# A graph attention kernel's first projection: pairs of tiles multiplied by seven half products instead of eight

## The chip, the cores and the metric

The kernel runs on one core of a Trainium2 chip. The core has five engines that run side by side, each with its own in-order queue of instructions: TensorE (PE) multiplies matrices into PSUM, VectorE (DVE) and ScalarE (ACT) work on tiles of 128 partitions, GpSimd (POOL) does so too and issues the indirect DMAs (gathers and scatters by an index), and SyncE (SP) issues most other DMAs. Engines wait for each other through semaphores.

The metric is the device time of one execution in microseconds. Before the change its median is 5629.17 us over 13 runs, the lowest 5609.52, the highest 5641.94.

## The reference, cut to what matters

Two graph attention layers over N = 10000 nodes and 170000 edges (each node has an edge to itself), with norms and residuals:

```
h0 = x                                            # 10000 x 768, float32
xl    = x @ W1                                    # W1 768 x 1024: 4 heads of 256
a_src = sum over a head of xl * a_src1            # one number per node and head
a_dst = sum over a head of xl * a_dst1
e     = leaky_relu(a_src[src] + a_dst[dst], 0.2)
alpha = softmax of e over the edges with the same dst
h     = segment_sum(xl[src] * alpha, dst) + b1
h     = relu(layer_norm(h)) + h0 @ Wr1 + br1
... the second layer in the same way, with W2, Wr2 and one head of 768 ...
out   = layer_norm(x + h)
```

The list of edges comes sorted by `dst`.

## The kernel before, in words

Nodes are taken in tiles of 128; 10000 nodes are NT = 79 tiles, numbered 0 to 78. The program has three stages, one after the other: the projection (described here), `ordered_layer1` and `ordered_layer2`. Between the first and the others stands a branch: every engine reads the number `fits` (written at L421 by the last step of the sorting) and goes on only then (L1232, L1234).

**The projection** is the loop at L659. For tile t it multiplies the transposed x (`xT`, 128 x 6 x 128, loaded by SP in `load_x`, L615, three buffers, two tiles ahead) by `w1` (six blocks of 128 x 1024). `product` (L164) issues 12 matmuls of 128 x 512, six for each half of the 1024 columns, into one of two PSUM tiles `big`; all is float32, and the profile shows two PE records for each such matmul. Then, for the same tile:

- ACT copies the product from PSUM to `row` (L662);
- DVE multiplies the product by `ad_b` and then by `as_b` into `scr` (L665, two buffers), and ACT sums each of the 4 heads of both with an accumulating activation (L668, 8 of them);
- POOL adds the bias `b1_b` to `row` (L670);
- SP issues the load of x for tile t + 2 (L671) and stores `row` to the DRAM table `table1` (L672);
- `next(steps)` (L673) issues one more step of two other pieces of work.

The order within each engine is the order in which this Python code issues the instructions (`manual_schedule`).

**The steps** are two generators taken side by side, `prepare` first and then `weight_steps`.

`weight_steps` (L632) loads W2 and, in 16 steps, multiplies one block of it by an attention vector on DVE (L647) and sums it on ACT (L648); then it multiplies `br1` by W2 on PE (L651) and evicts that on ACT (L653).

`prepare` (L190) sorts the nodes by their number of edges and finds where each node's edges are. Its parts, in order, are: loading the ends of the edge list; eleven transposes on PE (L216); 27 steps of **counts**; a one-hot matrix `hot` and 79 running additions `before` on DVE (L271, L276); ranks (L323 to L330, PE and DVE, eight tiles at a time); **scatters** of 79 columns to `order_d` by POOL (L313, six in a step); four loads back and the store `less_rank` on SP (L344, L347); and 20 steps of **slots**: POOL gathers `window` for four tiles (L392) and DVE, a step later, works out the slots from them (`listed`, L365).

A step of counts (L235 to L250) does three counts, each a DVE comparison of 1408 numbers with an accumulated sum (L239); converts them to integers `at` (L241); POOL gathers three `chunk` rows by `at` (L244); and DVE counts within the chunks of the step before (`remainder`, L228).

Of the kernel before, what the change touches and what calls it, by code (L numbers as in the profile page):

```python
# [28 lines left out]
F32 = mybir.dt.float32  # L29
I32 = mybir.dt.int32  # L30
BF16 = mybir.dt.bfloat16
AF = mybir.ActivationFunctionType
OP = mybir.AluOpType
AX = mybir.AxisListType

P = 128
# [43 lines left out]
def gnn_kernel(ctx, tc, x, x_cols, src, dst, src_col, dst_col, W1, a_src1, a_dst1, b1, g1, be1, Wr1, br1,  # L80
# [109 lines left out]
    def prepare():  # L190

        with tc.tile_pool(name="prep", bufs=1, side="right") as pool, \
                tc.tile_pool(name="prep2", bufs=2, side="right") as pool2:
            rows = pool.tile([P, NA, P], I32, name="rows")
            nc.sync.dma_start(rows, bass.AP(tensor=dst.tensor, offset=0, ap=[[P, P], [P * P, NA], [1, P]]))
            nxt = pool.tile([P, NA, P], I32, name="nxt")
# [7 lines left out]
            fall = pool2.tile([P, NA * P], F32, name="less", bufs=1).rearrange("p (a e) -> p a e", e=P)  # L204
# [9 lines left out]
            for a in range(NA):  # L214
# [6 lines left out]
                           allow_small_or_imprecise_dtypes=True)  # L221
            whole = pool.tile([P, NB], F32, name="whole")
# [10 lines left out]

            asked = []
            for j in range(0, NB, STEP):  # L235
                m = min(STEP, NB - j)
                for i in range(j, j + m):
                    less = pool2.tile([P, NA * P], F32, name="less", bufs=1)
                    nc.vector.tensor_scalar(less, most.rearrange("p a e -> p (a e)"), ids[:, i:i + 1], 0.0,  # L239
                                            op0=OP.is_lt, op1=OP.add, accum_out=whole[:, i:i + 1])  # L240
# [32 lines left out]
            before = pool.tile([P, NT + 1, D], BF16, name="before")  # L273
# [12 lines left out]
            facts = pool.tile([P, NT, 4], I32, name="facts")  # L286
# [11 lines left out]
            while s < D:  # L298
                more = pool.tile([P, D], F32, name=f"more{s}")
# [20 lines left out]
            for j in range(0, NT, W):  # L320
# [4 lines left out]
                place = pool2.tile([P, W, D], F32, name="place", bufs=1)  # L325
# [15 lines left out]
            others = [pool.tile([P, NT, 4], I32, name=n) for n in ("rows", "nxt", "info")]  # L341
# [23 lines left out]
            def listed(t, window):  # L365
# [3 lines left out]
                have, got, eq = (pool2.tile(shape, F32, name=n, bufs=1)[:, :m, :k] for n in ("have", "got", "eq"))  # L369
# [237 lines left out]
    with tc.tile_pool(name="w1", bufs=1) as w1p, tc.tile_pool(name="l1", bufs=2) as io, \  # L607
            psum_for_products(), tc.manual_schedule():
# [3 lines left out]
        def load_x(t):  # L612
            if t < NT:
                xTs[t] = io.tile([P, K0, P], F32, name="xT", bufs=3)
                nc.sync.dma_start(xTs[t], x_cols[t])  # L615
# [4 lines left out]
        load_x(1)  # L620
# [11 lines left out]
        def weight_steps():  # L632
# [7 lines left out]
            brT = spread_br1(w1p, "brT")  # L640
# [10 lines left out]
            q = product(brT, w2, R2)  # L651
            row = io.tile([P, R1], F32, name="row")
            nc.scalar.copy(row[:, :R2], q[:, :R2])  # L653
# [5 lines left out]
        for t in range(NT):  # L659
            p = product(xTs.pop(t), w1, C1)  # L660
# [625 lines left out]
```

## Time and profile before

| what | value |
|---|---|
| median of 13 runs | 5629.17 us |
| the profiled execution | 5638.83 us, span 5637.0 us |
| mean granted TensorE clock | 0.924 |
| projection, first to last matmul of L171 with `xT` | 8.9 to 872.0 us |
| matmul records of the projection | 1896 (79 tiles x 12 x 2) |
| eviction L662 of tile 0 and of tile 78 | start at 23.12 and 872.63 us |
| DVE L665, 128 x 1024 | 1.22 us each |
| ACT L668, 128 x 256 with a sum | 0.40 us each |
| DVE count L239, 128 x 1408 | 1.68 us each, 80 of them |
| POOL bias addition L670 | 2.37 us each |
| first instruction of the next stage on POOL (L424) | 882.1 us |

How it is read: times are of one execution, counted from the start of the span. A line of a timeline gives the start, the duration, engine, line of the code, operation, output and inputs with their shapes, and in brackets how long the engine had been idle before it and what released it. A line of the stretches gives each engine's busy time in the stretch, then the clock that TensorE was granted (1.00 is full), the DMA engines' busy share and GB/s. "xN" merges N records that follow each other.

### The profile page before, as it was taken

The page shows a single profiled execution, that of the slowest core. Times are in us where ns is not written, and L with a number is a line of the kernel's source. Part 1 is how long each engine was busy: PE and PEld are TensorE (multiplying, and loading weights), DVE is VectorE, ACT ScalarE, POOL GpSimd, SP SyncE. Part 2 cuts the span into 40 slices and gives each one's busy share as a digit, 9 for nine tenths or more (in the row PEclk, how much of TensorE's full clock was granted, in tenths as well). Part 3 has the DMA queues.
Part 4 walks back from the last instruction along what each step waited for, and adds up shares of the span by engine and source line. Part 5 has one row for each costly group of instructions (what it writes and reads, how often), then busy time and mean ns, then how long its engine had stood idle before and what let it go on. Part 6 is the DMA issues. An engine that isn't in the chain of part 4 may idle for free. (4 is left out here: it accounts for less than half of the span.)

```text
span 5637.0 us, 59565 instructions
## 1 busy us (share of the span) xinstructions
PE 4915.2 (87%) x15188; PEld 2905.0 (52%) x15191; DVE 4289.6 (76%) x7729; ACT 2811.1 (50%) x8184; POOL 3243.1 (58%) x3159
## 2 busy tenths in 40 slices
PE   8999996999999866789999998998878758788898
PEld 3444443555555544455555555655555435455565
DVE  5883344999999887888999995886776566677787
ACT  3443344777787766778777772332222222222232
POOL 3447454556666655566666544666666556666563
PEclk9999997999999987899999999998888768888899
DMA  4333526899999986999999977988888878888885
GB/s 155 122 98 87 94 94 260 319 336 353 362 367 368 350 318 246 332 348 360 364 363 351 337 260 272 334 322 307 300 293 289 279 255 286 300 302 299 289 325 197
DMA packets 474306, 1591.37 MB, mean 282 GB/s; under 512 B 118327, under 2 KB 122487, under 8 KB 473958
## 3 DMA queue, kind: packets, MB, share of 16 engines
q0 software_dynamic: 322384, 1286.62, 64.0%
q1 hardware_dynamic: 149520, 297.43, 15.5%
q10 hardware_dynamic: 2054, 3.42, 0.2%
q8 instruction: 128, 2.10, 0.1%
q14 instruction: 220, 1.80, 0.1%
HBM read 1431.80 MB, written 177.29 MB: 285 GB/s over the span
## 5 line engine op out<-in xcount | busy, mean ns | idle before, releaser
L424 POOL DMA_INDIRECT ring<-table,slots x2675 | 2661.1, 995 | 1801.0 <-issue 531.9
L519 DVE SCALAR_TENSOR_TENSOR acc<-ring,e,acc 128x512 f32<-128x512 f32 (+1 forms) x2530 | 1578.3, 624 | 149.3 <-PE acc L733 45.4
L508 ACT ACTIVATE ring<-ring,e 128x256 f32<-128x256 f32 x3284 | 1338.3, 509 | 2.3 <-issue 2.2
L952 PE MATMUL big<-wr,w 128*128 128x512 f32 (+1 forms) x2464 | 905.7, 511 | 176.9 <-issue 175.3
L515 DVE TENSOR_TENSOR acc<-acc,ring 128x1024 f32<-128x1024 f32 x801 | 985.7, 1231 | 72.5 <-DVE acc L519 1.8
L938 PE MATMUL big<-ring,diagonals 128*128 128x256 f32 x2754 | 744.3, 430 | 170.3 <-issue 120.9
L171 PE MATMUL big<-w,xT 128*128 128x512 f32 x1896 | 823.8, 596 | 23.0 <-DMA w<-in_W_dram 10.3
L171 PE MATMUL big<-wr,xT 128*128 128x512 f32 x1896 | 832.5, 596 | 0.2 <-issue 0.2
L826 PE MATMUL half<-w,hT 128*128 128x512 f32 (+1 forms) x2528 | 830.4, 486 | 0.0
L952 PEld LDWEIGHTS big<-wr,w 128*128 128x128 f32 x2464 | 489.4, 200 | 556.9 <-issue 524.8
L938 PEld LDWEIGHTS big<-ring,diagonals 128*128 128x128 f32 x2754 | 589.9, 218 | 328.5 <-issue 193.5
L937 ACT ACTIVATE diagonals<-ident,e 128x128 f32<-128x128 f32 x1377 | 424.8, 388 | 648.8 <-remote 226.0
L826 PEld LDWEIGHTS half<-w,hT 128*128 128x128 f32 x2528 | 477.8, 189 | 372.3 <-issue 333.6
L733 PE MATMUL acc<-ring,diagonals 128*128 128x256 f32 x1912 | 479.3, 408 | 208.4 <-ACT diagonals L727 203.7
L171 PEld LDWEIGHTS big<-w,xT 128*128 128x128 f32 x1896 | 361.3, 191 | 481.0 <-issue 462.5
L171 PEld LDWEIGHTS big<-wr,xT 128*128 128x128 f32 x1896 | 356.6, 191 | 419.8 <-issue 419.8
L733 PEld LDWEIGHTS acc<-ring,diagonals 128*128 128x128 f32 x1912 | 386.7, 205 | 293.8 <-ACT diagonals L727 225.2
L581 ACT ACTIVATE sd<-mv,eps 128x1 f32<-128x1 f32 x237 | 69.4, 293 | 706.7 <-DVE mv L579 468.7
L727 ACT ACTIVATE diagonals<-ident,e 128x128 f32<-128x128 f32 x956 | 293.0, 387 | 204.7 <-DVE e L499 179.9
L665 DVE TENSOR_TENSOR scr<-big,ad_b 128x1024 f32<-128x1024 f32 x79 | 96.7, 1224 | 374.6 <-ACT row L662 311.1
L670 POOL TENSOR_TENSOR row<-row,none 128x1024 f32<-128x1024 f32 x79 | 187.3, 2370 | 259.4 <-ACT row L662 256.0
L485 ACT ACTIVATE e<-e 128x68 f32<-128x68 f32 (+29 forms) x160 | 38.2, 239 | 564.2 <-DVE e L484 313.2
(173 smaller groups left out, 3639.8 us busy)
## 6 DMA issues: line engine op xcount, KB each, us to landing
ring<-table,slots POOLq DMA_INDIRECT x2675
table<-row SPq DMA_DIRECT2D x79, 516.0 KB
h_d<-hT SPq DMA_DIRECT2D x79, 512.0 KB
w<-h_d SPq DMA_DIRECT2D x77, 512.0 KB
table<-row SPq DMA_DIRECT2D x79, 385.0 KB
ring<-table SPq DMA_DIRECT2D x79, 385.0 KB
xT<-in_x_cols_dram SPq DMA_DIRECT2D x79, 384.0 KB
x_d<-xt SPq DMA_DIRECT2D x79, 384.0 KB
```

The lines of the kernel that those rows point to most:

```text
L171: nc.tensor.matmul(p[:, c:e], aT[:, j, :], w[:, j, c:e], start=(j == 0), stop=(j == k - 1))
L424: nc.gpsimd.indirect_dma_start(out=to, out_offset=None, in_=table, in_offset=bass.IndirectOffsetOnAxis(ap=index, axis=0), **more)
L508: nc.scalar.activation(row[:, s], row[:, s], AF.Copy, scale=e[:, h:h + 1])
L515: nc.vector.tensor_add(acc[:, :c], acc[:, :c], row[:, :c])
L519: nc.vector.scalar_tensor_tensor(acc[:, s], row[:, s], e[:, h:h + 1], (acc if first is None else first)[:, s], op0=OP.mult, op1=OP.add)
L670: nc.gpsimd.tensor_add(row[:, :C1], row[:, :C1], b1_b)
L727: nc.scalar.activation(diagonals[:, k * H1 + i, :], ident, AF.Copy, scale=e[:, k, i:i + 1])
L733: nc.tensor.matmul(acc[:, c:d], diagonals[:, k * H1 + i, :], ring.slot(q + k)[:, c:d], start=(k == 0 and c % BANK == 0), stop=(k == m - 1 ...
L826: nc.tensor.matmul(q, hT[:, j, :], w2[:, j, c:c + q.shape[1]], start=(j == 0), stop=(j == K1 - 1))
L937: nc.scalar.activation(diagonals[:, k % G, :], ident, AF.Copy, scale=e[:, k, :])
L938: nc.tensor.matmul(to, diagonals[:, k % G, :], ring.slot(FIRST[t] + k)[:, ON_PE2:C2], start=False, stop=(k == n - 1), skip_group_check=True)
L952: nc.tensor.matmul(r[:, c:d], hT[:, j, :], wr2[:, j, c:d], start=False, stop=(j == K1 - 1 and d < C2), skip_group_check=True)
```

## The change

Tile 0 is multiplied as before (by halves of the columns). After it the tiles are taken in pairs (1, 2), (3, 4) to (77, 78). The two tiles' x and W1 form 2 x 2 blocks: x's blocks are a11, a12 (tile t, first and second 384 of the inner dimension) and a21, a22 (tile t + 1); W1's are b11, b12, b21, b22 (halves of the inner dimension by halves of the columns). A half product is one such block by one such block, three matmuls of 128 x 512. Eight half products give the pair's result; the change uses Strassen's form with seven, of sums of blocks. b12 - b22 and b21 - b11 replace b12 and b21 in place, three more sums are kept in `bsums` (DVE, once), and five sums of x's blocks are made for each pair on DVE (`sums`, in `pair`), one pair ahead. The half products land in PSUM tiles of one bank, six of them. Two are evicted by ACT into `row` (m5 and m2); all others are added to or subtracted from `row` by DVE. `finish` is what came after the product before; it now reads `row` instead of PSUM, and each step follows one `finish`, so two steps are issued in a pair.

x has four buffers instead of three and is loaded for the tiles t + 4 and t + 5 ahead of the pair's stores; `row` has four buffers instead of two. Counts are issued one step ahead of the conversion that uses them, and those with an even number run on ACT: an accumulating Sign and a small activation that turns the sum of signs into a count. This adds one step to `prepare`. Several tiles of the sorting share storage under common names. `br1`'s product goes to the new PSUM tiles, two banks one after the other.

```diff
-            rows = pool.tile([P, NA, P], I32, name="rows")
+            both = pool.tile([P, 2, NA, P], I32, name="hot")
+            rows, nxt = both[:, 0], both[:, 1]
...
+            halves = pool.tile([P, NB], F32, name="halves")
+            nc.vector.tensor_scalar_add(halves, ids, -0.5)
...
+            def counts(j):
+                for i in range(j, min(j + STEP, NB)):
+                    less = pool2.tile([P, NA * P], BF16, name="less")
+                    if i % 2:
+                        nc.vector.tensor_scalar(less, most.rearrange("p a e -> p (a e)"), ids[:, i:i + 1], 0.0,
+                                                op0=OP.is_lt, op1=OP.add, accum_out=whole[:, i:i + 1])
+                        continue
+                    nc.scalar.activation(less, most.rearrange("p a e -> p (a e)"), AF.Sign, scale=-1.0,
+                                         bias=halves[:, i:i + 1], accum_out=whole[:, i:i + 1])
+                    nc.scalar.activation(whole[:, i:i + 1], whole[:, i:i + 1], AF.Copy, bias=0.5 * NA * P, scale=0.5)
+
             asked = []
+            counts(0)
+            yield
             for j in range(0, NB, STEP):
                 m = min(STEP, NB - j)
-                for i in range(j, j + m):
-                    less = pool2.tile([P, NA * P], F32, name="less", bufs=1)
-                    nc.vector.tensor_scalar(less, most.rearrange("p a e -> p (a e)"), ids[:, i:i + 1], 0.0,
-                                            op0=OP.is_lt, op1=OP.add, accum_out=whole[:, i:i + 1])
+                counts(j + STEP)
                 nc.vector.tensor_copy(at[:, j:j + m], whole[:, j:j + m])
...
-            others = [pool.tile([P, NT, 4], I32, name=n) for n in ("rows", "nxt", "info")]
+            others = [pool.tile([P, NT, 4], I32, name=n) for n in ("hot", "most", "info")]
...
-                xTs[t] = io.tile([P, K0, P], F32, name="xT", bufs=3)
+                xTs[t] = io.tile([P, K0, P], F32, name="xT", bufs=4)
...
-        for t in range(NT):
-            p = product(xTs.pop(t), w1, C1)
-            row = io.tile([P, R1], F32, name="row")
-            nc.scalar.copy(row[:, :C1], p[:, :C1])
+        def finish(t, row):
             for i, vec in enumerate((ad_b, as_b)):
                 m = io.tile([P, C1], F32, name="scr")
-                nc.vector.tensor_mul(m, p[:, :C1], vec)
+                nc.vector.tensor_mul(m, row[:, :C1], vec)
                 for h in range(H1):
...
             nc.gpsimd.tensor_add(row[:, :C1], row[:, :C1], b1_b)
-            load_x(t + 2)
             nc.sync.dma_start(table1[t * P:(t + 1) * P, :R1 - 1], row[:, :R1 - 1])
...
+        def times(a, b, p=None):
+            to = ps_m.tile([P, BANK], F32, name="m")[:, :NH] if p is None else p
+            for k in range(a.shape[1]):
+                nc.tensor.matmul(to, a[:, k, :], b[:, k, :], start=(p is None and k == 0),
+                                 stop=(k == a.shape[1] - 1), skip_group_check=True)
+            return to
...
+        def pair(t):
+            a1, a2 = (xTs.pop(i) for i in (t, t + 1))
+            a11, a12, a21, a22 = (a[:, k, :] for a in (a1, a2) for k in (upper, lower))
+            sums = io.tile([P, 5, KH, P], F32, name="sums")
+            for i, (a, op, b) in enumerate(((a11, OP.add, a12), (a21, OP.add, a22), (a11, OP.add, a22),
+                                            (a21, OP.subtract, a11), (a12, OP.subtract, a22))):
+                nc.vector.tensor_tensor(sums[:, i], a, b, op=op)
+            return a11, a22, sums
+
+        ready = pair(1)
+        for t in range(1, NT, 2):
+            a11, a22, sums = ready
+            r1, r2 = new_row(), new_row()
+            m3 = times(a11, b12)
+            m5 = times(sums[:, 0], b22)
+            nc.scalar.copy(r1[:, right], m5)
+            m2 = times(sums[:, 1], b11)
+            nc.scalar.copy(r2[:, left], m2)
+            nc.vector.tensor_sub(r2[:, right], m3, r2[:, left])
+            m4 = times(a22, b21)
+            nc.vector.tensor_sub(r1[:, left], m4, r1[:, right])
+            nc.vector.tensor_add(r1[:, right], r1[:, right], m3)
+            nc.vector.tensor_add(r2[:, left], r2[:, left], m4)
+            load_x(t + 4)
+            load_x(t + 5)
+            if t + 2 < NT:
+                ready = pair(t + 2)
+            m1 = times(sums[:, 2], bsums[:, 0])
+            nc.vector.tensor_add(r2[:, right], r2[:, right], m1)
+            m6 = times(sums[:, 3], bsums[:, 1])
+            nc.vector.tensor_add(r2[:, right], r2[:, right], m6)
+            times(sums[:, 4], bsums[:, 2], m1)
+            finish(t + 1, r2)
+            nc.vector.tensor_add(r1[:, left], r1[:, left], m1)
+            next(steps, None)
+            finish(t, r1)
             next(steps, None)
```

The seventh half product is added by PE onto the fifth (m1) in the same PSUM tile, after DVE has added m1 alone to r2. The step issued after `finish(t + 1)` is called step A in the text that follows, the one after `finish(t)` step B.

## The prediction

> **What bounds the kernel now.** I read the page first, then busy time by stretch of the projection (tile 78's last product matmul is issued at 872 us), then the timeline engine by engine inside each stretch.
>
> ```profile
> span 5637.0 us, 59565 instructions
> ...
> PE 4915.2 (87%) x15188; PEld 2905.0 (52%) x15191; DVE 4289.6 (76%) x7729; ACT 2811.1 (50%) x8184; POOL 3243.1 (58%) x3159
> ```
> ```profile
> core 0: us, PE busy (x) PEld busy (x) DVE busy (x) ACT busy (x) POOL busy (x), PEclk, DMA share, GB/s
> ...
> 75.00:257.00 182.00, 174.50 (x411) 77.07 (x410) 147.79 (x190) 81.06 (x302) 87.49 (x64) 1.00 0.35 118
> 257.00:372.00 115.00, 115.00 (x269) 50.92 (x268) 92.30 (x119) 48.35 (x188) 57.67 (x43) 1.00 0.33 107
> ...
> 436.00:640.00 204.00, 203.89 (x481) 90.28 (x482) 60.57 (x69) 82.85 (x328) 121.04 (x97) 1.00 0.45 93
> 640.00:872.00 232.00, 228.31 (x530) 100.87 (x529) 108.12 (x437) 94.94 (x374) 127.59 (x101) 0.99 0.36 90
> ```
> The projection is bound by PE: busy 100% from 257 to 372 us. But DVE is busy 80% there and 81% in the stretch before, because the sorting's counts lie beside the product. The average of 76% hides that: after 436 us DVE has 30%. In the first stretch PE is already held up, and the timeline shows by what:
>
> ```profile
> 128.38 0.84 ACT L648 ACTIVATE scr<-scr 128x768 f32<-128x768 f32 x1 [5.02 <-DVE scr L647]
> 129.13 0.18 ACT L648 ACTIVATION_READ_ACCUMULATOR scr<-scr 128x1 f32 x1
> 129.22 0.99 ACT L662 COPY row<-big 128x1024 f32<-128x1024 f32 x1
> ```
> ```profile
> 176.05 1.22 DVE L665 TENSOR_TENSOR scr<-big,ad_b 128x1024 f32<-128x1024 f32 x1 [1.90 <-ACT row L662]
> ...
> 178.32 1.67 DVE L239 TENSOR_SCALAR_CACHE_REDUCE less<-most,ids 128x1408 f32<-128x1408 f32 x1
> ...
> 180.03 1.68 DVE L239 TENSOR_SCALAR_CACHE_REDUCE less<-most,ids 128x1408 f32<-128x1408 f32 x1
> ```
> ```profile
> 167.05 10.54 PE L171 MATMUL big<-w,xT 128*128 128x512 f32 x24 [0.91 <-PE big L171]
> 178.50 10.54 PE L171 MATMUL big<-w,xT 128*128 128x512 f32 x24 [0.91 <-PE big L171]
> ```
> ACT works in order, so the eviction (L662) stands behind the step's L648, which waited for DVE; DVE then waits for the eviction, and PE loses 0.91 us. A tile takes 11.45 us here, 10.30 where PE is free (24 records, 0.429 us each). Evictions queued behind a step's work on ACT are thus a real bound, and the change puts more there.
>
> **The change part by part.** Pairs are named by their first tile: 39 pairs, tiles 1 to 78. All durations are of the profiled execution (5638.83 us; 9.7 above the median 5629.17, so I carry a difference over to the median).
>
> *Removed.* A half product is 6 records x 0.429 = 2.57 us. A pair had 8 (20.6 us) and has 7: 18.0. If PE set the pace, 39 x 2.57 = 100 us would go.
>
> *Added on DVE, per pair.* Five sums of 384 columns at 0.55 us (row L230), starting 0.47 apart: 2.45. Seven operations on 512 columns at 0.69 (rows L326, L328), 0.60 apart, 0.72 where one reads the one before: 4.6. Four multiplications of 1024 at 1.14 apart as before: 4.7 (from SBUF now; L665 reads PSUM in 1.22, so I change nothing). That is 11.6 against 4.7 before. Evictions on ACT: two of 512 at 0.59 (row L706) for two of 1.01.
>
> *Counts.* 80 counts at 1.72 us (L239 start to start) lay on DVE; 40 stay. One on ACT: L668 is 0.40 for 256 columns and L648 0.84 for 768, so 1.39 for 1408; a per-partition operand adds 0.11 (L508 0.51 against 0.40), and a small Copy that waits for the accumulator 0.3: 1.8. Between 1.4 and 2.2. Step A (after tile t+1) has two counts on DVE and one on ACT, step B (after tile t) one and two.
>
> *The new waits.* The order within a pair is now: PE may start the seventh product only when DVE has added the fifth to r2; ahead of that add DVE has four additions, the five sums, and ahead of those the wait for ACT's eviction of the third product, which is queued behind step B. Going once round from that add, in the pairs with counts: r2 += sixth 0.72, two multiplications 2.36, r1 += seventh 0.60, step A 4.70 (3.44 + 0.11 + 1.15), multiplication for t 1.22; ACT's eight accumulations 3.2, step B's two counts 3.6, two evictions 1.1; DVE's four additions 2.6, sums 2.45, the add 0.7. Sum 23.2 us, where before had 20.6 (257 to 372 us). With the W2 steps, 0.87 more on DVE (step A) and 0.85 on ACT (step B): 24.9 against 22.9. PE's 18.0 is hidden under it. Behind the delayed add on DVE stand all the multiplications that ACT's accumulations and POOL's bias additions wait for.
>
> *Steps A and B.* They were 10.3 us apart and are now 5 and 13. A step issues POOL's gathers and the next step uses them. For the slots (20 steps): POOL's bias addition starts 3.1 after the add, takes 2.4, four gathers start 1.26 apart (L392): last issue over at 10.3. DVE reaches step B at 8.9 and has to wait for landing.
>
> ```profile
> 693.36 0.95 POOL L392 DMA_INDIRECT window<-in_src_dram,begin  x1 [0.31 <-issue]
> 694.61 0.95 POOL L392 DMA_INDIRECT window<-in_src_dram,begin  x1 [0.30 <-issue]
> ...
> 698.63 2.37 POOL L670 TENSOR_TENSOR row<-row,none 128x1024 f32<-128x1024 f32 x1 [3.07 <-ACT row L662]
> ```
> Here the user starts at 701.02 without waiting, so landing takes 0 to 5.4 us after the last issue. A scatter of the same 128 rows was waited for twice in 79 (4.5 us after its issue; the others were under 4.2). I take 2.5, since most of these small transfers showed no wait. Then step B resumes at 12.8, its rest takes 2.6, additions, sums and add 5.75: 21.2 per pair, against 20.6. Each us of landing moves it by 1, ten pairs: -25 to +29 us. The Trainium skill (DMA: Bandwidth & Descriptors, Anatomy of one DMA) fits 2.0 us fixed for a GpSimd DMA; an estimate from that page would lower my sum by 5 us. No row here shows it.
>
> *Light pairs.* Fourth product over at 12.9 + 0.24, then 0.60 + 0.72 + 0.60 + 2.45 + 0.70: 18.2, so 18.4 with PE's restart.
>
> *Stalls over 18.0, summed.* Pair 1, W1's sums and differences (five of 1536 columns, 1.75) and sums behind them: 4.5. Pair 3, the eleven transposes (before: 19.0 for one tile): 7. Pairs 5 to 17: 6 x 6.9, less where ACT is not yet late: 42. Pairs 19, 21: 2 x 5.2, plus br1's product 10.6, plus 4 for its evictions and lift in the queues: 25. Pairs 23 to 31: 24. Pairs 33, 35 (hot 5.4, 79 additions at 0.22, lower 2.3 on DVE): 22. Pairs 37, 39 (ranks, 2.3 a group): 6. Pairs 41 to 57: 4. Pairs 59 to 75: 32. Total 167; 39 x 18.0 + 167 = 869 us for tiles 1 to 78. Before needed 849.5 (first eviction 23.1, last 872.6). So +20. After the last product, before has fits 4.0 us later (876.4); now r1's addition, two multiplications, the last slots and the check come behind it: 9.5. So +25.
>
> *Clock.*
> ```profile
> 654.58 25.71 PE L171 MATMUL big<-w,xT 128*128 128x512 f32 x56 [3.69 <-DMA xT<-in_x_cols_dram]
> ```
> ```profile
> 420.00:424.00 4.00, 3.70 (x10) 1.80 (x10) 3.62 (x17) 2.32 (x12) 0.16 (x1) 1.00 0.26 102
> ...
> 654.00:658.00 4.00, 3.42 (x5) 1.66 (x6) 1.58 (x5) 2.58 (x14) 3.25 (x4) 0.57 0.67 251
> ```
> After an idle 3.69 us PE's clock was 0.57 for some 3.3 us; after 3.21 us (at 420.3) it stayed 1.00. Above, PE idles 5 to 7 us a pair in some 14 pairs, and the seventh product, which DVE's addition waits for, follows at once: 1.6 us a pair if cold. Bounds 0 and 14 x 1.6 = 22; I take 15, nearer the row with the longer gap. The Trainium skill (TensorE: Matmul & The Clock Gate, Part 1: The HAM clock gate) has a free-running 3.4 us window, so that 5 us idle goes cold in about half of cases; that would be an estimate of 11.
>
> *Costed at nothing.* x a pair further ahead: covered by 18 us of lead; it also hides SP's 11.7 us block behind less_rank, whose 5.4 us stall (3.69 + half clock) lies in before's 849.5 and not in mine; without the cover +5. Six scatters a step: POOL 2 x (6 x 1.28 + 2.4) = 20.2 a pair against 18.4, 9 us late over five pairs; covered by four row buffers; without them +9. SP's stores now wait for POOL behind DVE's multiplications, still a pair ahead of the buffer's reuse. The sorting's tiles that share storage (hot, most, info): their earlier readers finish steps before; else one wait of some us. Table load for Sign: the row shows one load of 1.28 us, and the changed program's instruction order also has one ahead of all copies. Layers 1 and 2: same instructions, moved as a block.
>
> Sum: 20 + 5 + 15 = +40 us: 5679 against the profiled 5638.83; against the median 5629.17, **5669 us**.
>
> **The rivals.**
> *PE stays the bound (faster).* The place is ACT's queue between step B and the evictions: if those do not come late, pairs take 18.4 except the forced ones (br1, hot, transposes): 39 x 18.0 + 4.5 + 7 + 10.6 + 22 + 16 = 762, 87 less than before, tail +5: -82, 5547. It decides at a loop under 20.6 us. For it: PE 100% busy from 257 us. Against: the 0.91 us row, where a single L648 already reached PE.
> *Counts absorbed, slots not.* If the count loop is only DVE's 19.3 (21.1 with W2), 3.9 less in some 13 pairs, and hardly a cold gap: 40 - 50 - 5 = -15 at most, about 5622.
> *Loops as summed, no cold clock, quick landing.* +25 - 10: 5644.
> *Late landing and all gaps cold.* 4.5 us landing +20, clock +7: 5696.
>
> **How the numbers follow.** Chances: the forecast 0.50 (its own range 5655 to 5688), no cold clock and quick landing 0.20, late and cold 0.13, counts absorbed 0.09, PE-bound 0.08. Of the first three nearly all is slower by over 0.2% (11 us, about what a measurement here can tell from none): 0.79; absorbed counts split between faster and same, quick landing gives some same: faster 0.11, same 0.10. The range leaves out the PE-bound case and the extremes: 5622 to 5703.
>
> **What would show it.** After: fits 35 to 45 us later; DVE waiting for ACT's eviction of the third product in pairs 5 to 29, PE waiting 5 us before each seventh product there, clock under 1 in those stretches; DVE waiting for window only in step B; 18 us pairs between 520 and 680 us. It is wrong if ACT's counts take well under 1.8 us, or gathers land within 1 us, or PE shows no gaps.

## The result

The changed kernel is slower: 5705.59 us median (5692.64 to 5719.26, 7 runs) against 5629.17, a ratio of 1.0138 with a 95% interval of 1.0126 to 1.0151. That is +76 us where +40 was predicted (5669). The direction was right. The time lies 2.6 us above the range of 5622 to 5703.

The page of the changed kernel begins:

```profile
span 5702.4 us, 59691 instructions
...
PE 4856.5 (85%) x14954; PEld 2870.7 (50%) x14957; DVE 4573.7 (80%) x8123; ACT 2838.6 (50%) x8306; POOL 3267.0 (57%) x3159
```

PE has 59 us less work than before (4915.2), and DVE 284 us more (4289.6). In between stands the pace of the projection. These are the stretches that were shown of before, and the columns are the same:

```profile
core 0: us, PE busy (x) PEld busy (x) DVE busy (x) ACT busy (x) POOL busy (x), PEclk, DMA share, GB/s
75.00:257.00 182.00, 147.40 (x304) 62.91 (x303) 150.66 (x205) 98.50 (x327) 79.89 (x53) 0.90 0.25 86
257.00:372.00 115.00, 94.96 (x212) 41.91 (x210) 84.96 (x120) 55.97 (x184) 47.47 (x36) 0.93 0.33 115
436.00:640.00 204.00, 167.47 (x369) 71.91 (x371) 168.67 (x279) 61.24 (x272) 109.99 (x84) 0.92 0.24 72
640.00:872.00 232.00, 206.16 (x454) 88.50 (x453) 180.22 (x398) 83.30 (x374) 124.56 (x87) 0.94 0.47 93
```

PE was busy 174.50, 115.00, 203.89 and 228.31 us in them, at a clock of 0.99 to 1.00. Now it has gaps in every stretch and a clock of 0.90 to 0.94. From 436 to 640 us, where DVE had 60.57 us of work, it has 168.67.

POOL's first gather of the next stage starts at 965.5 us, 83.4 later than the 882.1 of before. What follows it took 4736.9 us against 4754.9, with the same instructions. In the runs below, on chips of about the same speed, this rest lay between 4721 and 4743, and it shows no tie to an edit of the projection. So I use this start as the measure of the projection, beside the ratio of whole times. It comes from one execution of each run, and a few microseconds of it are noise: pairs 1 to 55 of e4, which that run's edit leaves alone, took 2.6 us longer than in the changed kernel. The time of a pair is counted from its addition of m1 (L750) to that of the next pair. A pair with W2's steps takes up to 26.8 us, a pair with counts alone 24.2, a slots pair about 23, and only three pairs take the 18.2 of the unhindered loop.

DVE's waits in the projection of the changed kernel, then the wait of PE for the addition that has to precede the seventh product (who waited for whom: us in total, times, longest):

```profile
DVE row L740 <- ACT row L739: 50.1, 18, 5.2
DVE row L755 <- PE m L704: 35.8, 22, 2.4
DVE less L385 <- DMA window<-in_src_dram,begin: 30.9, 10, 5.6
...
PE m L704 <- DVE row L750: 123.5, 29, 12.1
```

Three of the predicted mechanisms are here: the evictions that come late behind step B (L739), PE's idle time ahead of the seventh product (L750), and the window that step B asks for too early (L385). The second line is the price of the clock: DVE waits up to 2.4 us for a seventh product that runs at half speed. Two seventh products of the PE timeline, after a long and after a short idle time:

```profile
134.93 5.49 PE L704 MATMUL m<-bsums,sums 128*128 128x512 f32 x6 [5.71 <-DVE row L750]
...
577.71 2.84 PE L704 MATMUL m<-bsums,sums 128*128 128x512 f32 x6 [1.18 <-DVE row L750]
```

And the stretches around them (granted clock 0.57 and 1.00):

```profile
134.00:142.00 8.00, 7.07 (x10) 2.97 (x11) 5.47 (x7) 4.96 (x19) 2.36 (x1) 0.57 0.06 26
569.00:580.00 11.00, 9.82 (x24) 4.14 (x23) 9.11 (x13) 0.67 (x2) 9.28 (x8) 1.00 0.38 119
```

Idle for 5.71 us, the six records take 5.49; idle for 1.18 us, 2.84. From DVE's addition of m1 (L750) to its addition of the seventh (L755) it is 3.78 to 3.88 us in 16 pairs and 4.9 to 6.3 in 23. The sum over the 23 is 39 us.

What no line of the prediction had is in the durations of DVE's own instructions. First the timeline of both engines around pair 47, then around a rank group:

```profile
614.73 0.68 DVE L744 TENSOR_TENSOR row<-row,m 128x512 f32<-128x512 f32 x1
615.32 5.32 DVE L728 TENSOR_TENSOR sums<-xT 128x384 f32<-128x384 f32 x5
...
616.00 2.35 POOL L694 TENSOR_TENSOR row<-row,none 128x1024 f32<-128x1024 f32 x1
```

```profile
546.84 2.59 DVE L342 CAST to<-rank 128x8 int32<-128x8 f32 x1
547.04 2.35 POOL L694 TENSOR_TENSOR row<-row,none 128x1024 f32<-128x1024 f32 x1
```

Five sums take 2.42 us when nothing is beside them. Here they take 5.32, and POOL's bias addition of 2.35 lies inside. A cast of eight columns, 0.17 us elsewhere, takes 2.59 and ends when POOL's addition does. The groups show how often (count: shortest/median/longest, ns):

```profile
L728 DVE TENSOR_TENSOR sums<-xT x195: 496/551/3450, 28.0 to 926.5; 128x384 f32<-128x384 f32 x195
...
L689 DVE TENSOR_TENSOR scr<-row,ad_b x79: 1209/1225/3562, 25.4 to 952.2; 128x1024 f32<-128x1024 f32 x79
L689 DVE TENSOR_TENSOR scr<-row,as_b x79: 1212/1218/3948, 26.5 to 955.1; 128x1024 f32<-128x1024 f32 x79
...
L253 DVE CAST at<-whole x27: 164/956/2986, 90.9 to 427.8; 128x3 int32<-128x3 f32 x26, 128x2 int32<-128x2 f32 x1
```

In the projection 47 instructions of DVE took over a quarter of a microsecond more than the shortest of their line and shape, 73 us more in all; before, it was 4 us in two. All but one of the 47 ran beside a bias addition of POOL. The multiplications of before read PSUM, and the longest of 158 was 1.225 us. An addition of 512 columns that reads PSUM (L740 to L755) is never stretched in the changed kernel either (0.674 to 0.693).

### The profile page after: what moved, and what is told of

Same layout as the page of the kernel before. It is cut to its first block, busy times and chain, and to the rows that moved or that the text cites. A ratio compares the mean times of both kernels' runs of the same rounds, so it can differ in the third digit from the quotient of the medians.

```text
span 5702.4 us, 59691 instructions
## 1 busy us (share of the span) xinstructions
PE 4856.5 (85%) x14954; PEld 2870.7 (50%) x14957; DVE 4573.7 (80%) x8123; ACT 2838.6 (50%) x8306; POOL 3267.0 (57%) x3159
## 5 line engine op out<-in xcount | busy, mean ns | idle before, releaser
L692 ACT ACTIVATE scr<-scr 128x256 f32<-128x256 f32 x632 | 253.5, 402 | 485.3 <-DVE scr L689 454.4
L704 PE MATMUL m<-bsums,sums 128*128 128x512 f32 x702 | 360.3, 665 | 123.5 <-DVE row L750 123.5
L704 PEld LDWEIGHTS m<-bsums,sums 128*128 128x128 f32 x702 | 144.0, 210 | 325.1 <-issue 166.4
```

Of the source, the lines that this page charges most:

```text
L704: nc.tensor.matmul(to, a[:, k, :], b[:, k, :], start=(p is None and k == 0), stop=(k == a.shape[1] - 1), skip_group_check=True)
```

## The experiments

Theory: three things make the pairs long, and they lie in different pairs: ACT's evictions behind step B (Q), the clock that goes cold ahead of the seventh product (C), and DVE's instructions with two operands in SBUF that stand still while POOL reads SBUF (L). The rivals are named with each run. Ratios are against the kernel before, timed beside each run on the same chip; the changed kernel stands at 1.0138. "Start" is the start of POOL's first gather of the next stage in the profiled execution (965.5 in the changed kernel, 882.1 before).

| run | edit | ratio (95%) | start, us |
|---|---|---|---|
| e1 | no bias addition | 1.0100 (1.0071 to 1.0130) | 943.0 |
| e2 | POOL writes only | 1.0088 (1.0065 to 1.0111) | 938.6 |
| e3 | PE kept warm | 1.0091 (1.0065 to 1.0117) | 943.4 |
| e4 | slots two steps later | 1.0109 (1.0088 to 1.0131) | 960.0 |
| e5 | step B behind the evictions | 1.0086 (1.0060 to 1.0112) | 934.4 |
| e6 | e4 and e5 | 1.0050 (1.0033 to 1.0066) | 919.4 |
| e7 | eight half products, the rest as changed | 0.9994 (0.9979 to 1.0008) | 880.7 |
| e8 | counts on DVE alone | 1.0204 (1.0179 to 1.0229) | 994.7 |
| e9 | e6, bias by PE | 0.9961 (0.9946 to 0.9975) | 868.0 |
| e10 | e9 and lighter steps | 0.9928 (0.9911 to 0.9944) | 853.9 |
| e11 | e7, br1 early | 0.9962 (0.9948 to 0.9976) | 869.0 |
| e12 | e2 and e3 | 1.0067 (1.0050 to 1.0084) | 922.0 |

e9, e10 and e11 ran on a chip on which the kernel before takes 5330 us, not 5621 to 5638 as in the other runs; their medians are to be read by the ratio only. Their starts can be compared: an unhindered tile takes 10.3 us in e11 as in e7, and the 300 us lie in what follows the start (4433 to 4440 us).

**POOL's reading: e1 and e2.**

```diff
-            nc.gpsimd.tensor_add(row[:, :C1], row[:, :C1], b1_b)          # e1: left out
+            for _ in range(2):                                            # e2: in its place
+                nc.gpsimd.memset(row[:, :C1], 0.0)
```

> The changed kernel with POOL's 79 bias additions (2.36 us each, 128x1024) left out; the table lacks b1, everything else stays. Theory L (a DVE instruction with both operands in SBUF, or a cast, stands still while POOL's addition reads SBUF): in the changed kernel DVE's instructions of the projection took some 75 us longer than the shortest of their kind (sums 15, multiplications 17, casts 27, the rest 16), before 3 us; they fall back to their shortest, and the time falls by 35 to 60 us (5646 to 5671). Rival Q (only POOL's queue matters: the window gathers stand behind the addition in ten pairs): 10 x 2.4 = 24 us less at most, 5682, and DVE's instructions are as long as before. Rival N (the additions are beside everything): 0 +- 6.

> The changed kernel with each bias addition replaced by two POOL memsets of the same row (128x1024 each), which wait for the same multiplications and write SBUF but read nothing; the stored rows are zeros. Theory L in the form 'it is POOL's reading that blocks DVE's second operand': the sums and multiplications keep their shortest time (0.48 and 1.21 us), casts may still wait; 15 to 35 us less than the changed kernel, 5670 to 5690, if the two memsets last about 2.4 us together. In the form 'any POOL instruction on SBUF blocks': no difference, 5706 +- 6. Rival Q: no difference if POOL is occupied as long.

In e2 the groups of DVE and the memsets are:

```profile
L729 DVE TENSOR_TENSOR sums<-xT x195: 494/553/610, 28.0 to 902.5; 128x384 f32<-128x384 f32 x195
...
L689 DVE TENSOR_TENSOR scr<-row,ad_b x79: 1209/1225/1226, 25.4 to 928.6; 128x1024 f32<-128x1024 f32 x79
L689 DVE TENSOR_TENSOR scr<-row,as_b x79: 1212/1219/1227, 26.5 to 930.2; 128x1024 f32<-128x1024 f32 x79
...
L253 DVE CAST at<-whole x27: 163/299/1565, 90.9 to 428.2; 128x3 int32<-128x3 f32 x26, 128x2 int32<-128x2 f32 x1
...
L695 POOL MEMSET row<- x158: 951/952/981, 27.9 to 932.5; 128x1024 f32 x158
```

No sum and no multiplication is stretched any more; only casts still are, by less. The 73 us are 4. The start comes 26.9 us earlier, inside the 15 to 35 that were expected of "it is POOL's reading". POOL is occupied 1.9 us in two memsets instead of 2.36, so at most 0.9 us a pair could be owed to that. The gain lies where DVE's instructions were long, and is larger: the pairs from 41 to 51 took 19.5 to 22.7 us and now take 18.2 to 18.3. The pairs with W2's steps stay at 25.7 to 26.8, although a cast in each had been stretched by 1.6 us: other waits take the gain back there, so not every stretched instruction cost time.

The Trainium skill (SBUF — State Buffer, Who interferes with whom) says that VectorE and GpSimd share one pair of ports as an exclusive lock, that a VectorE instruction with two inputs in SBUF contends with a GpSimd instruction that reads SBUF and not with one that only writes, and that copies and casts in a two-port mode contend as well. These two runs agree: 73 us against 4 with writing alone, all of it in casts.

e1 misses its range on the small side (22.5 us of 35 to 60), although no DVE instruction is stretched there at all. One pair shows why: pair 37 took 57.2 us (26.7 in the changed kernel). SP's issues there (a merged line runs from the start of its first issue to the end of its last; each issue takes 0.33 us):

```profile
512.23 11.23 SPq L694 DMA_DIRECT2D table<-row  x2
530.89 28.39 SPq L629 DMA_DIRECT2D xT<-in_x_cols_dram  x2
```

The two stores lie as far apart in the changed kernel (10.94 us), but its loads lie 5.2 us apart and these 28. In the same time ACT's evictions wait 18.5 and 7.1 us, and from 540 to 560 us PE does nothing and the DMA engines move 3 GB/s. The profile doesn't show what they wait for. POOL, with no addition between its steps, issues 38 scatters there between 505 and 556 us, mostly 1.27 us apart; but e9 issues them nearly as densely (43 in 60 us against 46), and the two loads of a pair start at most 5 us apart there. So the scatters alone do not explain it, and the cause stays open. Outside of this pair e1 gains some 50 us, which the stretched instructions and the earlier gathers explain: the slots pairs take 18.2. The times of e1 spread more than those of any other run here (5639 to 5701).

**The clock: e3.**

```diff
             m6 = times(sums[:, 3], bsums[:, 1])
+            for _ in range(FILL.get(t, 0)):          # 1 or 2 in 24 pairs
+                fill = ps_tr.tile([P, BANK // P, P], F32, name="tr").rearrange("p a b -> p (a b)")
+                for k in range(KH):
+                    nc.tensor.matmul(fill, sums[:, 3, k, :], bsums[:, 1, k, :], start=(k == 0), stop=(k == KH - 1))
```

> The changed kernel with one or two extra half products for nothing (3 matmuls of 128x512 each, 2.6 us, into the PSUM tile that the sorting's transposes use) ahead of the seventh half product, in the 24 pairs where PE idled over 2.5 us there. Theory C (clock): the seventh half products that ran after such an idle time took 1.1 to 2.5 us longer than the 2.74 us of the others, 39 us in 23 pairs, and DVE's addition that waits for each stands in the loop that sets the pace; kept warm, they take 2.74 and the time falls by 25 to 39 us, 5667 to 5681. Rival (the loop is closed elsewhere, by ACT's queue or DVE's stretched instructions): 0 to -8 us, the wait for the seventh product turns up as another wait.

Work for nothing on the engine that Strassen was to relieve makes the kernel faster: the start comes 22.1 us earlier, the ratio is 0.0047 lower (26 us; 25 to 39 were expected). The time from the addition of m1 to that of the seventh product is 3.8 us in every pair with counts now, and the excess over it has fallen from 39 us in 23 pairs to 15 in 9: five are still cold, in three the fill itself holds the product up, in one a stretched multiplication does. PE's wait for DVE, in the same view as above (line numbers move with the edits; L752 here is L750 of the changed kernel):

```profile
PE m L704 <- DVE row L752: 45.5, 23, 8.7
```

The pairs with W2's steps take 24.3 us instead of 26.8. So the clock is worth 2.5 us in each of them. The same run shows the price of a fill that isn't needed: pairs that had become light take 20.6.

Which idle times lose the clock can be read from the profiles, as the granted clock changes only on a fixed grid of 3.41 us. Four stretches of that grid in the changed kernel, around the seventh products of pair 31 (2.48 us idle, went cold) and pair 75 (3.30 us idle, stayed at full clock):

```profile
420.99:424.40 3.41, 1.40 (x4) 0.68 (x5) 3.27 (x6) 0.00 (x0) 0.00 (x0) 1.00 0.08 29
424.40:427.81 3.41, 3.41 (x6) 1.35 (x5) 2.36 (x4) 2.77 (x14) 1.44 (x1) 0.50 0.00 0
...
922.75:926.16 3.41, 1.63 (x4) 0.38 (x2) 3.38 (x8) 0.00 (x0) 1.39 (x2) 1.00 0.07 5
926.16:929.57 3.41, 1.89 (x5) 0.93 (x6) 3.27 (x5) 0.00 (x0) 0.00 (x0) 1.00 0.00 0
```

In pair 31 the idle time falls into one stretch, PE is busy 1.40 of its 3.41 us, and the next stretch runs at half clock. In pair 75 it is shared by two, each busy for 1.63 us or more, and the clock stays. In the first 960 us of the 14 profiles, all 213 full-clock stretches with PE busy under 40% were followed by half clock, and 3164 of the 3172 with 45% or more by full clock; the other eight lie at the eleven transposes. By these numbers one idle time under 1.9 us cannot lose the clock by itself, one over 4.1 us always does, and between them its place on the grid decides.

**Clock and lock together: e12**, with both edits.

> The changed kernel with POOL writing zeros into the rows instead of adding the bias, and with the extra half products that keep PE warm, in one. If the stretched DVE instructions and the cold clock are two separate causes, their gains add: the next stage starts on POOL at 965.5 - 26.9 - 22.1 = 916 us (910 to 925), about 49 us under the changed kernel. If they share the same loop, the second gives little: 930 us or later.

922.0: together 43.5 us of the 49 that they win apart, within the expected range. Three pairs whose fill is needless without the stretched instructions (45, 47, 51: 20.6 us instead of 18.2) cost 7 us. Over the whole projection the two causes add up nearly in full. They are not separate everywhere: pair 45 falls from 22.7 us to 18.2 or 18.3 by either edit alone.

**Step B and the window: e4, e5, e6.**

```diff
+                asked.append((t, window))            # e4
+                if len(asked) > 2:
+                    listed(*asked.pop(0))
-                for r in asked:
-                    listed(*r)
-                asked = [(t, window)]
```

```diff
             nc.scalar.copy(r2[:, left], m2)          # e5
+            if t > 1:
+                next(steps, None)
...
             finish(t, r1)
-            next(steps, None)
```

> The changed kernel with the slots of a group worked out two steps after its gathers instead of one (the window has three buffers already). Theory W (step B waits for gathers that step A issued 8.9 us earlier): DVE's 30.9 us of waits for window, in 10 pairs, go; 20 to 31 us less, 5675 to 5686. Rival (the wait only moves, to POOL's four gathers a step or to ACT's evictions): 0 to -8 us.

> The changed kernel with step B issued after the next pair's two evictions (L737, L739) instead of before them, so that on ACT the evictions come ahead of the step's counts; on DVE nothing changes place. Theory Q (the evictions' place behind step B's two counts on ACT closes the loop in pairs 5 to 29): DVE's wait for the eviction of the third product (50 us in all) mostly goes, a pair with counts takes DVE's own 19.5 us (21.3 with W2's steps) plus what the cold seventh product adds, 1.5 to 3.5 us less in 13 pairs: -25 to -45 us, 5661 to 5681. Rival (the cold clock and DVE's stretched instructions carry it): -10 us at most.

> Both: step B after the next pair's evictions, and the slots two steps after their gathers. If the two causes lie in different pairs (5 to 31 and 57 to 77) their gains add: -45 to -75 us, 5630 to 5660. If the clock or the stretched DVE instructions carry either stretch, less than 30 us.

e5 does what was expected of it: 31.2 us. The wait for the eviction falls from 50.1 to 30.9 us only, but what is left lies in pairs 1, 5 and 21 and in the light pairs 43 to 57; in the other pairs with counts it is gone:

```profile
DVE less L385 <- DMA window<-in_src_dram,begin: 34.1, 10, 9.9
DVE row L757 <- PE m L704: 31.7, 20, 2.4
DVE row L742 <- ACT row L739: 30.9, 10, 5.2
```

The pairs with W2's steps take 22.0 to 23.5 us (26.8), those with counts alone 20.4 to 21.9 (24.2): the loop through ACT's queue is real, and its edit wins more than any other single one. A part of that is the clock: in pairs 11 and 25 to 31 the seventh product now stays at full speed.

e4 misses by the start. No wait for the window is left, and yet the start comes only 5.5 us earlier. Pair 57, where the first slots wait for the first gathers, wins 4.8 us, and the nine pairs after it 0.7 each; the end of the projection loses 2.6 again, and 2.6 are the noise named above. By the ratio of whole times the gain is 16 us, but with an interval of 2 to 30. In the other slots pairs DVE now stands still in one of the next instructions instead. DVE and then POOL, in e4:

```profile
800.13 2.29 DVE L386 TENSOR_TENSOR less<-less,below 128x80 f32<-128x80 f32 x1
...
799.87 2.44 POOL L694 TENSOR_TENSOR row<-row,none 128x1024 f32<-128x1024 f32 x1 [0.40 <-issue]
```

L386, with both operands in SBUF, takes 0.24 us alone and 2.29 beside POOL's addition. In the whole projection such delays rise from 73 to 84 us. The wait for the window had hidden that. So the rival was right that the wait moves, and wrong on where to. With step B later as well (e6) the sum is 46.1 us, at the lower end of what was expected.

**Strassen and the counts: e7, e8, e11.**

> The changed kernel without Strassen: each tile multiplied by its 12 matmuls of 128x512 into a two-bank PSUM tile and multiplied by the vectors from PSUM, as before, with the rest of the change (counts on ACT and a step ahead, four x and four row buffers, x loaded four tiles ahead of the stores). If all the loss comes from the seven half products and what they bring: the 5.4 us stall behind less_rank goes, and DVE's lighter count steps give up some of 16 x 1.15 us: 5600 to 5625. If counts on ACT cost by themselves (their 1.7 us stand ahead of the evictions on ACT): 5640 to 5680.

> The changed kernel with all counts on DVE again (a step ahead as changed; none on ACT). In pairs 5 to 31 DVE then has 0.72 + 2.36 + 0.6 + 6.4 + 2.36 + 6.4 + 2.6 + 2.45 + 0.7 = 24.6 us of its own (26.4 with W2's steps) against measured 24.2 (26.8) with the evictions behind ACT's counts. Theory Q (the loop through ACT's queue is as long as DVE's own): the same within 10 us, 5696 to 5716. Rival (ACT's counts as such are the fault): 25 us less or more, under 5681.

> Without Strassen, with the rest of the change, and br1 spread for its product early again and its sum a step later. In the run without Strassen, tile 20 took 32.0 us instead of 14.1 because PE waited 8.7 us for that spreading and DVE 13.5 us for the sum; the other tiles saved 1.15 us each in 16 tiles. If these are the two sides of its zero, 15 to 20 us now show: 5600 to 5617. Rival (the layers after it take it back, or another wait comes): 5622 or more.

```diff
-                    if i % 2:                        # e8
+                    if True:
```

```diff
+        for t in range(NT):                          # e7, in place of the pairs
+            p = product(xTs.pop(t), w1, C1)
+            row = new_row()
+            nc.scalar.copy(row[:, :C1], p[:, :C1])
+            load_x(t + 4)
+            finish(t, row, p)                        # multiplies from p, in PSUM
+            next(steps, None)
```

Without Strassen the rest of the change is worth nothing measurable (0.9994), and the start is 1.4 us earlier than before. All of the loss thus comes with the seven half products. The zero has two sides. Tiles 6 to 19 take 10.3 us instead of 11.4 to 11.5, and the stall behind less_rank is gone (tile 58: 15.7 before, 10.3 now). Against that, tile 20 took 32.0 us instead of 14.1 (from eviction to eviction, as all tile times here). PE's line of it, then DVE's:

```profile
236.16 13.01 PE L671 MATMUL m<-w,scr 128*128 128x512 f32 x32 [8.73 <-DVE scr L614]
```

```profile
249.62 0.16 DVE L674 TENSOR_TENSOR lift<-row 128x1 f32<-128x1 f32 x1 [13.51 <-ACT row L673]
```

The change spreads br1 just before its product, behind DVE's counts (a line of the change that the extract above leaves out), and lets DVE wait 13.5 us for the sum lift. e11 spreads it early again and adds lift a step later: tile 20 takes 20.6 us, and the kernel is faster than before (0.9962). Of the expectation for e7, the mechanism of its faster case was right and tile 20 had been left out.

e8 misses: I held ACT's counts to be as long a detour as DVE's own, and expected no difference. With all counts on DVE the start is 29.2 us later, and the pairs with W2's steps take 28.5 to 29.6 us. The 26.4 that were worked out for DVE's own loop leave out the wait for the cold seventh product, up to 2.4 us; together 28.8. Stretched instructions have no part in it: e8 has none in these pairs. ACT's counts help this kernel.

**All of it: e9 and e10.** In e9 PE adds b1, as one bfloat16 matmul of 128x512 each behind the first and the fourth half product (b1 in three bfloat16 parts, in 32 rows each against a weight of 1/32). These two reach each quarter of the pair's result once. ACT's accumulations take the constant off again that b1 adds to a head's sum.

```diff
-            nc.gpsimd.tensor_add(row[:, :C1], row[:, :C1], b1_b)
...
+            if bias is not None:                     # in times(); m3: right, m4: left
+                nc.tensor.matmul(to, share, bs[:, bias], start=False, stop=True, skip_group_check=True)
...
-                    nc.scalar.activation(m[:, s], m[:, s], AF.Copy,
+                    nc.scalar.activation(m[:, s], m[:, s], AF.Identity, bias=less_b[:, i * H1 + h:i * H1 + h + 1],
                                          accum_out=row[:, C1 + i * H1 + h:C1 + i * H1 + h + 1])
```

e10 adds:

```diff
-                    if i % 2:
+                    if i % 3 == 1:                   # two of three counts on ACT
...
-                if j // W % 2:
-                    write(known)
-                    known = j + m
-                    yield
+                write(known)                         # one rank group a step
+                known = j + m
+                yield
...
+            yield                                    # lift a step later
             nc.vector.tensor_add(lift, row[:, C2:C2 + 1], row[:, C2 + 1:R2])
```

> Step B after the evictions, slots two steps after their gathers, and POOL's bias addition replaced: PE adds b1 to the first and the fourth half product (one bfloat16 matmul of 128x512 each, b1 in three bfloat16 parts), and ACT's accumulations take the constant that this adds to the attention sums away again. Theory L: of the 46 us that step B's place and the slots won, this keeps all and adds the 27 us that the write-only run won, less at most 39 x 0.45 = 17 us on PE: next stage from 885 to 905 us on POOL (882 before, 919 with the two reorderings alone), 5630 to 5655. Rival (POOL's scatters, no longer spaced by additions, hold up SP's stores and loads as in the run without bias, 33 us in one pair): no better than 5660.

> As the run before it, and: two of three counts on ACT (instead of one of two), the rank groups one a step instead of two, and the sum lift a step after br1's product. Theory (DVE's and ACT's work per pair, as measured, sets the pace once nothing blocks): count pairs lose one count on DVE, 1.7 us in 13 pairs; rank pairs fall from 25.6 to about 20 us, three of them; lift's 12.6 us wait goes: another 30 to 45 us, 5590 to 5625, below the kernel before. Rival (the clock and SP's held-up stores take it back): 5630 or more.

e9 is better than expected: the start is at 868.0 us (885 to 905), 14 before the kernel before. No DVE instruction is stretched, most light and slots pairs take 18.6 us, and with fewer gaps the clock went cold in 6 pairs instead of 23. The rival falls: no pair shows the stop of e1's pair 37. e10 brings it to 853.9, with a ratio of 0.9928: faster than both kernels. Its stretches:

```profile
75.00:257.00 182.00, 165.84 (x367) 71.24 (x373) 151.06 (x229) 139.32 (x406) 46.72 (x45) 0.94 0.36 123
257.00:372.00 115.00, 109.39 (x264) 49.16 (x267) 89.16 (x137) 83.53 (x250) 33.18 (x33) 1.00 0.31 98
436.00:640.00 204.00, 201.54 (x479) 87.68 (x485) 143.61 (x220) 99.30 (x374) 84.38 (x79) 0.99 0.44 97
```

PE is the bound again from 436 to 640 us (201.54 of 204 us), with most pairs at 18.6 to 19.5 us there; the pairs with W2's steps, in the first stretch, take 20.8. Of the 100 us that seven half products save on PE, 15 are left against the start of e11, which has eight; and e10's lighter steps have a part in these.

## Why the prediction was right or wrong

- **What bounds the kernel, and the direction.** Right. The evictions behind step B's work on ACT were named as the bound that the change would run into; e5 shows 31 us for them. The loop of a pair with W2's steps was put at 24.9 us without the clock, and it measures 26.8 with it and 24.3 with the clock kept warm (e3). With counts alone 23.2 was worked out, and 22.6 measured warm.
- **Multiplications from SBUF, "so I change nothing".** This is the step that failed. Each multiplication's own duration is unchanged when it runs alone (1.22 us), but the sums and the multiplications now read two operands from SBUF, and so do the steps' instructions that had other neighbours before. Beside POOL's addition they stand still: 73 us in DVE's durations, 27 us at the end (e2). The multiplications of before, from PSUM, could not show a price. But a row of before does, which I had costed at 0.22 us an addition: two of the 79 additions L276, which read both operands from SBUF, took 2.23 and 2.27 us where the shortest took 0.18, each beside a bias addition of POOL. The second, and POOL's addition:

```profile
397.30 2.27 DVE L276 TENSOR_TENSOR before<-before,hot 128x64 bf16<-128x64 bf16 x1
...
397.18 2.35 POOL L670 TENSOR_TENSOR row<-row,none 128x1024 f32<-128x1024 f32 x1 [12.28 <-ACT row L662]
```

  So the term could have been given bounds: nothing, or up to 2.1 us for each of POOL's 79 additions. It is also why the pairs from 41 to 51 did not take 18.4 us. The stalls over 18.0 of the pairs 41 to 57 were put at 4 us and measure 25. Of these, 16 in the pairs 41 to 55 went in e2; 7 are pair 57's wait for the first gathers.
- **Clock, "bounds 0 and 14 x 1.6 = 22; I take 15".** Right in kind, and the bound was too low in both factors: 23 pairs instead of 14, 1.1 to 2.5 us each, 39 us of longer seventh products, of which keeping PE warm wins 22. I had taken the two rows of before (3.21 us idle kept the clock, 3.69 lost it) for a limit. Idle times of 2.48, 2.60 and 2.73 us lost it in the changed kernel, while 3.30 us did not; the grid under e3 shows why. The 15 idle times of 4.16 us and more all went cold, so the lower bound 0 and the 15 were too low for gaps of 5 to 7 us. The Trainium skill (TensorE: Matmul & The Clock Gate, Part 1: The HAM clock gate) has the clock fall after about one idle window of 3.4 us; these shorter times went cold all the same, and the measurement decides. For the same reason the estimate that half of the 5 us gaps go cold did not hold here.
- **Slots, "landing 2.5".** The waits for window are there in step B alone, 30.9 us in 10 pairs. As the price of the slots pairs they were the smaller half: without them the pairs were only 0.7 us shorter (e4), since the stretched instructions stood behind the wait. 21.2 us a pair were predicted and 20.7 to 23.5 came.
- **Counts, 1.8 us on ACT.** 1.45 us for the activation, and 1.7 from start to start: a good bound, and the counts helped by 29 us (e8).
- **x loaded further ahead, costed at nothing.** Right: no stall at less_rank in e7, as in the changed kernel. "br1's product 10.6 and 4 for its evictions" was close for the pairs 19 and 21 (25 us over 18.0 predicted, 24.6 measured). But e7 and e11 show, with eight half products, that 11 us came with where the change spreads br1 and adds lift, and the prediction named the first of these nowhere.
- **The sum.** Predicted for the end of the projection were 20 + 5 + 15 = 40 us, and 83 came. The lock is 27 of the missing 43 and the clock 7 (22 for 15). With both taken away (e12), the start is 40 us after that of before, where the prediction without its clock term had 25; 7 of those 40 are needless fills. Some 8 us in the rank pairs (37 and 39: 16 us of stalls where 6 were put) and in small terms stay unassigned. Two sums were off in themselves: the pairs 59 to 75 are nine, not ten, so 29 us and not 32; and the -15 of absorbed counts gives 5614, not 5622.
- **The rivals.** "PE stays the bound" and "counts absorbed" fell with the shown loops, "no cold clock, quick landing" with the 23 cold pairs and the 30.9 us of waits for the window. "Late landing and all gaps cold" (5696) came nearest, for its second half.

## What to carry to other kernels

When an edit moves an operand of a VectorE instruction from PSUM to SBUF, look at what GpSimd does in the same microseconds; the instruction alone costs the same, and its neighbour may more than double it (1.22 us became up to 3.95). A faster product is worth its saving only in stretches that nothing else sets, so write the loop through every in-order queue once round before counting it: here seven eighths of PE's work gave a loop of 24 to 27 us in place of 21 to 23. And where PE idles for 2 us or more ahead of work that others wait for, price the clock with the idle time; work for nothing in the gap can be the cheaper choice.

## What the runs showed of the hardware that was not expected

- A cast of 3 columns on VectorE (0.16 us) took up to 2.99 us, beside a gather and then GpSimd's 2.36 us addition; with memsets, which only write, in place of the addition, up to 1.56 us, while additions and multiplications of VectorE were not touched by the memsets at all.
- It goes the other way too: 39 of GpSimd's 238 gathers and scatters in the projection took over 1.15 us, up to 3.30 instead of 0.95, and 35 of them ran mostly beside a multiplication with both operands in SBUF. Before, one did (1.57 us), beside L647, which reads both from SBUF as well.
- TensorE's clock went to half after idle times of 2.48 to 2.79 us (five of five in the changed kernel), and after 2.19 us in e3; it stayed full after 2.42 and once after 3.30 us. What decided was how much of one 3.41 us stretch of a fixed grid was idle.
- In e1 SyncE's two loads of pair 37 were issued 28 us apart while GpSimd issued scatters without a pause; in e9 scatters as dense had no such effect, and the cause was not found.
